# Layer 0 up to three blocks ahead of layer 1, handed out step by step, in half-block streams

## The chip, the cores and the metric

One core of one Trainium2 chip runs the whole program in one launch. The metric is the device time of that launch in microseconds (us), as the median of several runs. PE is the matmul engine, ACT the scalar engine (exponentials, copies with a scale), DVE the vector engine (reductions, elementwise), POOL the GpSimd engine, SP the queue that issues DMAs. SBUF is the on-chip memory that all engines read; PSUM holds eight banks of 128 x 512 fp32 into which PE alone writes its results.

## The reference

The input is x of shape (4, 2048, 256): four sequences ("batches") of 2048 tokens, 256 channels, fp32. Two layers follow each other, each with attention and a feed-forward part, each part added to x:

```python
x = x + attn0(layernorm(x))     # one head, key and value dim 64, biases, causal softmax
x = x + ffn0(layernorm(x))      # clip and round to fp8 (e4m3), to fp16, times W^T, + bias
x = x + attn1(layernorm(x))     # 16 heads of 16, rotary embedding of q and k, causal softmax
x = x + ffn1(layernorm(x))      # xr, xk = mixes of x and x one token earlier
                                # sigmoid(xr Wr^T) * (relu(xk Wk^T)^2 Wv^T)
```

Everything is per token except the two attentions, which look at all earlier tokens of the same sequence, and the last part, which looks one token back. Most of the work is the scores of layer 1: 16 heads, each 2048 x 2048, half of it cut off by the causal mask.

## The kernel before, in words

**Tiling.** A block is 512 tokens (`BLK`). Each of the 4 batches has blocks qb = 0 to 3, so there are 16 blocks in `order`, numbered i. Layer 1's attention goes block by block. The 16 heads form 4 groups g of 4 heads; the four heads of a group sit on the four 32-row strips of PE and run side by side. For one block and group the keys are walked in steps kt of 128 keys: 4, 8, 12 or 16 steps for qb = 0, 1, 2, 3. In all there are 4 x 4 x (4+8+12+16) = 640 such steps, and they are the main loop of the program.

**A step.** `scores` issues twelve matmuls into four PSUM banks (high half of q, low half of q, and the shift by the row maximum, for four heads; on the diagonal also mask matmuls). `exponentials` turns the four banks into probabilities on ACT, two heads at a time. `weighted` multiplies the probabilities of the step before with the values into the bank `av`. `maxima` issues eight matmuls into four more banks for a later group, and four DVE reductions (`reduce_max`, line 612) take their row maxima; a group's maxima must all be done before its scores start, because the softmax shift is a row of the score matmul (`shift_of`). Seven banks of PSUM rotate among scores, maxima and everything else; the eighth is `av`.

**Work beside the steps.** Everything else is written as Python generators that yield after each chunk an estimate of its PE time: `layer0` (layer norm, projections, maxima, scores and values of layer 0 for one block), `layer0_rest` (output projection, fp8 feed-forward, second layer norm and transposes, one generator for each half of the block), `project1` (q, k, v of layer 1, rotary embedding on POOL, split of q and k in high and low parts, transposes) and `layer1_end` (output projection, layer norm, token mix, feed-forward, output DMA). The first three form the list `first` for the next block, i+1, made by `first_part` when block i begins; `layer1_end` of block i-1 goes into the list `end` at the third step of block i. `beside` pulls from `first` while there is any, then from `end`.

**Order.** Python issues all instructions in one sequence, and at the end of `seq_kernel` each engine's instructions are tied to that order, so every engine works through its queue exactly as issued: an instruction that waits holds up all behind it on its engine. Within a step the chunks may come at up to three places, by the rate that is due: after the first two exponentials, after the last two, and behind the maxima. The rate spreads what is left over the remaining steps of the same block:

```python
rate = max(left, 0.0) / max((NG - g) * n - kt - 1, 1)
if first:
    rate = max(rate, early)
credit = min(credit + rate, rate + 2.0)
slots = 3 if rate > 3 else 2 if rate > 1.8 else 1
```

`run_maxima` issues a group's maxima during the group before, two steps ahead; before the first maxima of a new block it pulls what is left of `first` in one go, because those maxima need that block's q and k.

**Buffers.** SBUF tiles named `w2` (128 x 512 fp32, 10 of them) and `w4` (128 x 1024 fp32, 4) serve the chunks, `pT` (4 of 128 x 2 x 512) the probabilities, `x` (3 of 128 x 4 x 256) the activations of a block.

Of the kernel before, what the change touches and what calls it, by code (L numbers as in the profile page):

```python
# [22 lines left out]
P = 128  # L23
# [7 lines left out]
HG = 4  # L31
# [6 lines left out]
W2, W4, PT = 10, 4, 4  # L38


def turns(*gens):

    live = list(gens)
    while live:
        for g in list(live):
            try:
                yield next(g)
            except StopIteration:
                live.remove(g)
# [3 lines left out]
def seq_kernel(  # L53
# [63 lines left out]
    def load_x(b, qb):  # L117
        t = work.tile([P, TT, C], F32, tag="x", name=f"x_{b}_{qb}", bufs=3)
        nc.sync.dma_start(
            t, x_in[b, qb * BLK : (qb + 1) * BLK, :].rearrange("(t p) c -> p t c", p=P)  # L120
        )
        return t
# [82 lines left out]

    def bank(name, dtype=F32):
        cols = BLK * (2 if dtype == F16 else 1)
        return ps.tile([P, cols], dtype, tag="sc", name=name)
# [4 lines left out]
    def w2(name, dtype=F32):  # L213
        return work.tile([P, BLK], dtype, tag="w2", name=name, bufs=W2)
# [4 lines left out]
    def w4(name, more=0):  # L219
        return work.tile([P, CK * (BLK + more)], F32, tag="w4", name=name, bufs=W4)  # L220

    def w4n(name):
        return w4(name).rearrange("p (t c) -> p t c", t=TT)

    def w4t(name):
        return w4(name).rearrange("p (k n) -> p k n", k=CK)
# [3 lines left out]
    def stats(x, hf, tag):  # L230

        mv = small.tile([P, 2, 2], F32, tag="mv", name=f"mv_{tag}_{hf}")
# [6 lines left out]
        y = small.tile([P, 2], F32, tag="y", name=f"y_{tag}_{hf}")  # L239
# [29 lines left out]
    def normal_T(x, dst, hf, tag, copy):  # L269

        my = stats(x, hf, tag)
        yield 0.0
        xn = w2n(f"xn_{tag}_{hf}")
        normalize(x, hf, my, xn)
        yield 0.0
        transpose(xn, dst[:, :, hf * HALF : (hf + 1) * HALF], f"{tag}_{hf}", copy)
        yield 0.6
# [6 lines left out]
    def shift_rows(pad, name):  # L284
# [8 lines left out]
        sh = work.tile([P, BLK], F32R, tag="sh", name=name, bufs=3)  # L293
        nc.scalar.copy(sh, pt)  # L294
        return sh


    kT0, v0 = {}, {}

    def layer0(b, qb, x):  # L300
        tag = f"a0_{b}_{qb}"
        xT = w4t(f"xT_{tag}")
        yield from turns(
            normal_T(x, xT, 0, tag, nc.scalar.copy),
            normal_T(x, xT, 1, tag, nc.vector.tensor_copy),
        )
        kT = kv.tile([P, BLK], F32R, tag="kT0", name=f"kT_{tag}", bufs=NB)
        qh = w2(f"qh_{tag}", F32R)
        ql = w2(f"ql_{tag}", F32R)
        for i in range(2):  # L310
            pq = bank(f"pq_{tag}_{i}")
            for k in range(CK):
                nc.tensor.matmul(  # L313
                    pq, wqk0[:, k, i * P : (i + 1) * P], xT[:, k, :],
                    start=(k == 0), stop=(k == CK - 1),
                )
            hi = (qh, kT)[i]
            lo, r = ((ql, slice(0, P)), (kT, slice(D0, P)))[i]
            nc.scalar.activation(hi, pq, AF.Identity, bias=bqk[:, i : i + 1])
            nc.vector.scalar_tensor_tensor(  # L320
                lo[r, :], pq[r, :], bqk[r, i : i + 1], hi[r, :].bitcast(F32),
                ALU.add, ALU.subtract,
            )
            yield 1.8
        pv = bank(f"pv_{tag}")
        for t in range(TT):
            token_mm(pv[:, t * D0 : (t + 1) * D0], xT, wv0, t)
        va = kv.tile([P, TT, D0 + 1], F32, tag="v0", name=f"v_{tag}", bufs=NB)
        nc.vector.tensor_tensor(
            va[:, :, :D0],  # L330
            pv[:, : TT * D0].rearrange("p (t d) -> p t d", t=TT),
            bv_bc[:, None, :].to_broadcast([P, TT, D0]),
            ALU.add,
        )
        nc.gpsimd.memset(va[:, :, D0 : D0 + 1], 1.0)
        kT0[qb], v0[qb] = kT, va
        yield 1.8


        mx = small.tile([P, TT, NB], F32, tag="mx0", name=f"mx_{tag}")  # L340
        for t in range(TT):
            for kb in range(qb + 1):
# [10 lines left out]
                if kb % 2 or kb == qb:  # L353
                    yield 0.6 * (1 + kb % 2)
# [4 lines left out]
        sh = shift_rows(pads[2], f"sh_{tag}")  # L359
# [5 lines left out]
        for kt in range(nkt + 1):  # L365
            now = None
            if kt < nkt:
                sc = bank(f"s_{tag}_{kt}")
# [13 lines left out]
            if last is not None:  # L382
# [4 lines left out]
                )  # L387
            last = now
            yield 1.6
        cx = w2(f"cx_{tag}")[: D0 + 1, :]  # L390
        nc.scalar.copy(cx, av[: D0 + 1, :])
        ctx0[b, qb] = cx, work.tile(
            [P, CK, BLK], F16, tag="w2", name=f"qhT_{tag}", bufs=W2
        )
        yield 0.0

    ctx0, xT1, ready1 = {}, {}, set()

    def layer0_rest(b, qb, x, hf):

        tag = f"a0_{b}_{qb}"
        while (b, qb) not in ctx0 or (hf == 1 and (b, qb, 0) not in ready1):
            yield None
        cx, qhT = ctx0[b, qb]
        t2 = slice(2 * hf, 2 * hf + 2)
        if hf == 0:
            xT1[b, qb] = w4t(f"xT1_{tag}")
        for t in range(2 * hf, 2 * hf + 2):
# [8 lines left out]
            )  # L417
        my = stats(x, hf, f"f{tag}")
        yield 1.0
        ready1.add((b, qb, hf))  # L420
# [10 lines left out]
        for k in range(CK):  # L431
# [5 lines left out]
        nc.vector.tensor_copy(  # L437
            qhT[:, :, hf * HALF : (hf + 1) * HALF],
            pt[:, :BLK].rearrange("p (k n) -> p k n", k=CK),
        )  # L440
        yield 0.5
        po = bank(f"pof_{tag}_{hf}")
        for j in range(2):
            token_mm(po[:, j * C : (j + 1) * C], qhT, wf16, 2 * hf + j)
# [6 lines left out]
        yield from normal_T(  # L451
            x, xT1[b, qb], hf, f"a1_{b}_{qb}", (nc.scalar.copy, nc.vector.tensor_copy)[hf]
        )
        ready1.add((b, qb, hf, "T"))

    kT1, v1, q1 = {}, {}, {}
    VW = NH * (DK + 1) + SLOT - DK - 1

    def project1(b, qb, x):

        tag = f"a1_{b}_{qb}"
        while (b, qb, 0, "T") not in ready1:
            yield None
        xT = xT1[b, qb]

        va = kv.tile([P, TT, VW], F32, tag="v1", name=f"v_{tag}")
        nc.gpsimd.memset(va, 1.0)
        v1[b, qb] = va  # L470
        H2 = DK // 2
        roped = {}

        def project(t):
            it = qb * TT + t
            pq = bank(f"pq_{tag}_{t}")
            token_mm(pq, xT, wqkv1[:, :, : 2 * C], t)
# [3 lines left out]
            rb = w2(f"rb_{tag}_{t}")  # L481
            rb2 = rb.rearrange("p (h z d) -> p h z d", z=2, d=H2)
            for z, s in ((0, nsin_sb), (1, sin_sb)):
# [8 lines left out]
            nc.gpsimd.tensor_tensor(qk[:, C:], qk[:, C:], rb[:, C:], ALU.add)  # L492
            qd = w2(f"qd_{tag}_{t}")
            nc.gpsimd.tensor_tensor(
                qd.rearrange("p (h z d) -> p h z d", z=2, d=DK),
                *(
                    r[:, :C].rearrange("p (h d) -> p h d", d=DK)[:, :, None, :]
                    .to_broadcast([P, NH, 2, DK])
                    for r in (qk, rb)
                ),  # L500
                ALU.add,
            )
            roped[t] = qk, qd

        def values(t):
            pv = bank(f"pv_{tag}_{t}")
            token_mm(pv[:, :C], xT, wqkv1[:, :, 2 * C :], t)
# [3 lines left out]
            )  # L511

        def halves(t):
            qk, qd = roped[t]
            kn = w2(f"kn_{tag}_{t}", F32R)
# [6 lines left out]
            roped[t] = kn, qd  # L522

        def slots(t):
            kn, qd = roped.pop(t)
            cols = slice(t * P, (t + 1) * P)
            if t == 0:
                kT1[b, qb] = kv.tile([P, NG, BLK], F32R, tag="kT1", name=f"kT_{tag}")
                q1[b, qb] = [
                    [  # L530
# [451 lines left out]
```

## Time and profile before

| | |
|---|---|
| runs | 3714.28, 3714.72, 3714.59 us; median 3714.59 |
| profiled execution | 3709.86 us; span 3707.0 us, mean granted PE clock 0.893 |
| PE busy | 3272.5 us (88%) |
| DVE, ACT, POOL busy | 2068.7 (56%), 1671.8 (45%), 618.0 us (17%) |
| layer 1 score steps | 640; the first starts at 100.7 us |
| line 612, DVE, maxima | 2560 reductions, 1377.5 us |
| line 646, ACT, exponentials | 2560, 1167.1 us |
| line 624, PE, score matmuls | 7680, 1301.8 us in the three groups |
| line 653, PE, probabilities x values | 5120, 663.5 us |

An engine's busy time is the union of its instructions' times. Matmuls overlap in the pipeline, so a group's sum can exceed what it adds to the span. The granted clock is the share of full speed that PE's clock was let run at; in this trace it is at any moment 1.0 or 0.5, so 0.893 means that PE ran at half speed for 21% of the span. A stretch of the span can be asked for its busy times and its clock; the prediction does that block by block.

### The profile page before, as it was taken

What the parts mean: (1) busy time and instruction counts of PE and PEld (TensorE: products, weight loads), DVE (VectorE), ACT (ScalarE), POOL (GpSimd) and SP (SyncE); (2) the same over time, 40 slices, a digit from 0 to 9 for tenths busy, and PEclk for the clock granted to TensorE, in tenths of its full rate; (3) what the DMA queues carried; (4) which work ended last, traced back from release to release, by engine and by line L of the source; (5) the groups of instructions that cost most, each with busy time, mean ns of one, the idle gap of its engine ahead of it and who ended that gap; (6) DMA issues with size and microseconds to landing.
All of it is one profiled execution on the core that took longest, in us unless ns stands there. A gap on an engine that the chain in (4) does not pass through costs nothing.

```text
span 3707.0 us, 73056 instructions
## 1 busy us (share of the span) xinstructions
PE 3272.5 (88%) x31136; PEld 1708.1 (46%) x31136; DVE 2068.7 (56%) x4455; ACT 1671.8 (45%) x3552; POOL 618.0 (17%) x825
## 2 busy tenths in 40 slices
PE   4788898899979899899997979889997888988998
PEld 3454444444445454444454545444444544444444
DVE  3464655667445465656634556456754554646663
ACT  1234444455534444445643434454563434444455
POOL 3212103002030300301203030120211202021001
PEclk8788899799988889989997989998998898999899
DMA  1000000000000000000000000000000000000000
GB/s 52 1 1 1 13 1 1 12 1 2 13 1 12 1 13 1 1 13 2 2 13 1 13 1 13 1 1 13 2 4 10 13 1 4 9 1 7 1 1 12
DMA packets 22903, 24.63 MB, mean 7 GB/s; under 512 B 3953, under 2 KB 22322, under 8 KB 22578
## 3 DMA queue, kind: packets, MB, share of 16 engines
q1 hardware_dynamic: 22578, 19.97, 1.7%
q8 instruction: 244, 4.00, 0.5%
q14 instruction: 81, 0.66, 0.1%
HBM read 11.18 MB, written 8.39 MB: 5 GB/s over the span
## 4 chain that ended last, share of the span: by engine, by line
PE 68%; DVE 24%; ACT 3%; POOL 2%; issue 2%; DMA 0%; POOLq 0%; ACTq 0%; DVEq 0%
DVE mx L612 16%; PE s L624 15%; PE av L653 14%; PE m L599 9%; PE av_a L384 3%; PE pq_a L264 3%; PE pk_f L726 2%; ACT p L646 2%; PE pq_a L313 2%; PE s_a L372 2%; PE pw_f L264 2%; PE pr_f L264 2%; PE s L634 2%; PE pv_a L264 1%; PE m_a L346 1%
## 5 line engine op out<-in xcount | busy, mean ns | idle before, releaser
L612 DVE TENSOR_REDUCE mx<-m 128x1 f32<-128x512 f32 (+3 forms) x2560 | 1377.5, 602 | 932.9 <-PE m L599 594.5
L646 ACT ACTIVATE p<-s 128x512 f32<-128x512 f32 (+3 forms) x2560 | 1167.1, 541 | 1102.4 <-PE s L634 576.6
L624 PE MATMUL s<-qh_a,kT_a 32*128 32x512 f32 (+3 forms) x2560 | 592.0, 482 | 88.3 <-DVE mx L612 70.0
L653 PE MATMUL av<-p,v_a 128*32 128x512 f32 (+3 forms) x5120 | 663.5, 589 | 0.0
L624 PEld LDWEIGHTS s<-qh_a,kT_a 32*128 32x128 f32 x2560 | 267.4, 195 | 426.5 <-DVE mx L612 212.2
L599 PE MATMUL m<-kT_a,qh_a 32*128 32x512 f32 (+3 forms) x2560 | 391.2, 487 | 46.6 <-DVE mx L612 33.3
L599 PEld LDWEIGHTS m<-kT_a,qh_a 32*128 32x128 f32 x2560 | 173.7, 195 | 460.2 <-issue 167.5
L624 PE MATMUL s<-ql_a,kT_a 32*128 32x512 f32 (+3 forms) x2560 | 371.1, 431 | 0.0
L624 PE MATMUL s<-sh,ones 32*128 32x512 f32 (+3 forms) x2560 | 338.7, 395 | 0.0
L599 PE MATMUL m<-kT_a,ql_a 32*128 32x512 f32 (+3 forms) x2560 | 290.7, 394 | 0.0
L238 POOL TENSOR_SCALAR v_fa<-mv_fa 128x2 f32<-128x2 f32 x32 | 7.0, 219 | 1251.2 <-DVE mv_fa L236 1251.2
L624 PEld LDWEIGHTS s<-sh,ones 32*128 32x128 f32 x2560 | 204.4, 205 | 22.7 <-ACT sh L294 5.4
L653 PEld LDWEIGHTS av<-p,v_a 128*32 128x32 f32 x5120 | 108.6, 113 | 181.3 <-issue 161.5
L624 PEld LDWEIGHTS s<-ql_a,kT_a 32*128 32x128 f32 x2560 | 176.0, 203 | 0.0
L599 PEld LDWEIGHTS m<-kT_a,ql_a 32*128 32x128 f32 x2560 | 153.3, 201 | 0.0
L264 PE MATMUL pq_a<-wqkv,xT_a 128*128 128x512 f32 x256 | 140.6, 676 | 4.9 <-ACT xT_a L259 4.9
L384 PE MATMUL av_a<-p_a,v_a 128*65 128x512 f32 (+3 forms) x320 | 144.3, 533 | 0.2
L380 ACT ACTIVATE p_a<-s_a 128x512 f32<-128x512 f32 (+3 forms) x160 | 86.8, 542 | 97.0 <-PE s_a L375 57.5
L258 PE MATMUL pt_a<-ident,xn_a 128*128 128x128 f32 x256 | 55.8, 359 | 73.0 <-DVE xn_a L247 73.0
L634 PE MATMUL s<-maskT_p,ident_p 32*128 32x128 bf16 (+3 forms) x4096 | 119.5, 208 | 0.0
L352 DVE TENSOR_REDUCE mx_a<-m_a 128x1 f32<-128x512 f32 (+3 forms) x160 | 90.6, 604 | 47.2 <-PE m_a L346 41.3
L550 DVE TENSOR_TENSOR ql_a<-pt_a,qh_a 128x256 fp32r<-128x256 f32 x128 | 54.1, 423 | 105.6 <-ACT qh_a L549 105.6
(157 smaller groups left out, 3859.4 us busy)
## 6 DMA issues: line engine op xcount, KB each, us to landing
x<-in_x SPq DMA_DIRECT2D x16, 512.0 KB, 3.9
out_y<-x SPq DMA_DIRECT2D x32, 256.0 KB, 2.1
wqkv<-in_wqkv1T SPq DMA_DIRECT2D x1, 768.0 KB, 8.4
wqk<-in_wqk0T SPq DMA_DIRECT2D x1, 256.0 KB, 4.3
wo<-in_wo1T SPq DMA_DIRECT2D x1, 256.0 KB, 8.6
wr<-in_wrT SPq DMA_DIRECT2D x1, 256.0 KB, 8.8
wk<-in_wkT SPq DMA_DIRECT2D x1, 256.0 KB, 7.4
wv<-in_wvT SPq DMA_DIRECT2D x1, 256.0 KB, 6.0
```

The costliest lines, as they stand in the source:

```text
L264: nc.tensor.matmul(dst, lhsT[:, k, t * P : (t + 1) * P], w[:, k, :], start=(k == 0), stop=(k == CK - 1),)
L313: nc.tensor.matmul(pq, wqk0[:, k, i * P : (i + 1) * P], xT[:, k, :], start=(k == 0), stop=(k == CK - 1),)
L352: nc.vector.reduce_max(mx[:, t, kb : kb + 1], sc[:, :w], axis=AX.X)
L372: nc.tensor.matmul(sc[:, c0:], keys, qh[:, c0:], start=True, stop=False)
L380: nc.scalar.activation(pT[:, c0:], sc[:, c0:], AF.Exp, scale=D0**-0.5)
L384: nc.tensor.matmul(av[: D0 + 1, c:], v0[k // TT][:, k % TT, :], p[:, c:], start=(k == 0), stop=(k == nkt - 1),)
L599: nc.tensor.matmul(scs[h][:, :w], q[r, cols], kT1[b, kb][r, g, :w], start=(q is qh), stop=(kb < qb and q is ql),)
L612: nc.vector.reduce_max(mx[:, t, h, kb : kb + 1], scs[h][:, :w], axis=AX.X)
L624: nc.tensor.matmul(scs[h][:, c0:], ones[r, :] if i == 2 else kT1[b, kt // TT][r, g, kcols], sh[r, c0:] if i == 2 else (qh, ql)[i][r, c0:], ...
L634: nc.tensor.matmul(scs[h][:, c0 : c0 + (v + 1) * SLOT], ident_p[r, v, :], maskT_p[r, v, : (v + 1) * SLOT], start=False, stop=(v == HG - 1),)
L646: nc.scalar.activation(pTs[h // 2][:, h % 2, c0:], scs[h][:, c0:], AF.Exp, scale=DK**-0.5)
L653: nc.tensor.matmul(av[h * SLOT : (h + 1) * SLOT, c0:], v1[b, kt // TT][:, kt % TT, at : at + SLOT], pTs[h // 2][:, h % 2, c0:], start=(kt ...
```

## The change

- **Layer 0 runs ahead.** It is no longer tied to the next block. `a_of` makes its five generators for a block (two halves of `a_in`, `a_mid`, two halves of `a_out`), and `refill` starts the next block whenever the list `A` is empty, up to two blocks beyond the running one, or three once the end of the previous block is through. Before the first step, layer 0 of block 0 is done and that of block 1 partly. There are four `x` buffers.
- **Metering.** A step's credit grows by at least `BASE` = 1.75, more where the deadlines of `rate_of` ask for it. A generator whose chunk yields zero or more is pulled at most once in a step; a negative yield lets it go on in the same step.
- **Place.** All chunks stand behind the step's maxima, none between the exponentials.
- **Half-block streams.** `layer1_end` becomes `end_half`, once for each half; `project1` is split into `b_in`, `b_project`, `b_keys` and `b_queries`. q of layer 1 is kept in one tile `qr` and doubled on POOL (two copies) only when its pair of groups is due.
- **Maxima of a block's first group** are all issued during the last group of the block before, from its first step on; `force(Bq)` completes what they need in that step.
- **Buffers.** 13 `w2` and no `w4`; `pT` is 6 tiles for one head each; copies of transposed tiles are all on ACT.

The diff, cut to its core:

```diff
-W2, W4, PT = 10, 4, 4
+W2, PT = 13, 6
...
-        t = work.tile([P, TT, C], F32, tag="x", name=f"x_{b}_{qb}", bufs=3)
+        t = work.tile([P, TT, C], F32, tag="x", name=f"x_{b}_{qb}", bufs=4)
...
-        transpose(xn, dst[:, :, hf * HALF : (hf + 1) * HALF], f"{tag}_{hf}", copy)
+        if not out_to:
+            out_to.append(w2t(f"xT_{tag}_{hf}"))
+        transpose(xn, out_to[0], f"{tag}_{hf}", nc.scalar.copy)
+        done(1)
         yield 0.6
...
-            yield 1.6
+            yield -1.7
...
-            qd = w2(f"qd_{tag}_{t}")
-            nc.gpsimd.tensor_tensor(
-                qd.rearrange("p (h z d) -> p h z d", z=2, d=DK),
...
+            nc.gpsimd.tensor_tensor(qr1[b, qb][:, t, :], qk[:, :C], rbf[:, :C], ALU.add)
+            roped[b, qb, t] = count[0], qk, rb
+            yield -1.8
...
+    def b_keys(b, qb):
+        for t in range(TT):
+            while (b, qb, t) not in roped or count[0] < roped[b, qb, t][0] + 2:
+                yield None
...
+    def b_queries(b, qb, pair, hf):
...
+        qd = w2(f"qd_{tag}_{hf}")
+        for j in range(2):
+            nc.gpsimd.tensor_copy(
...
-    def layer1_end(b, qb, x, cn):
+    def end_half(b, qb, x, cn, hf):
...
-        for hf in range(2):
-            nc.scalar.activation(sg[:, hf * BLK : (hf + 1) * BLK], prs[hf], AF.Sigmoid)
+        sg = w2(f"sg_{tag}")
+        nc.scalar.activation(sg, pr, AF.Sigmoid)
         yield 1.8
...
-                yield G - 1 + (s + 1) / n - 2 / lead, i
+                yield G - 1 + (s * (lead - 1) // n / lead if g == 0 else (s + 1) / n - 2 / lead), i
...
+    def pull(lists, floor, once=True):
...
+                    if once and used.get(id(gen)) == count[0]:
+                        continue
...
+                    if c >= 0:
+                        used[id(gen)] = count[0]
+                    credit -= abs(c)
...
+    def refill(i):
+        if not A and a_next < min(i + (4 if not E and at[1] > 0 else 3), N):
+            a_load[0] = 0.0
+            A.extend(a_of(a_next))
+            a_next += 1
...
+    def rate_of(i, g, kt, n):
+        to = lambda where: max(where * n - (g * n + kt), 1)
+        rate = BASE
+        first = a_load[0] if a_next == i + 2 else 0.0
+        if first > 0 or Bq:
+            rate = max(rate, first / to(1.5), (first + b_load[0] + e_load[0] / 2) / to(3))
+        return max(rate, (q_load[0] + e_load[0]) / to(4))
...
+    while Bq or Q:
+        credit = 1.0
+        pull([Bq, Q, A], -1e9)
+        pull([A2], -4.0 if A else -6.0)
+        count[0] += 1
...
-            if need >= done_first:
-                pull(first)
+            if need > b_done:
+                force(Bq)
+                b_done = need
...
-            slots = 3 if rate > 3 else 2 if rate > 1.8 else 1
+            refill(i)
+            rate = rate_of(i, g, kt, n)
+            credit = min(credit + rate, rate + 1.5)
             scs, pTs, c0 = scores(b, qb, g, kt, shifts[G])
             exponentials((0, 1), scs, pTs, c0)
-            if slots > 2:
-                beside(credit - rate / 3)
...
             exponentials((2, 3), scs, pTs, c0)
-            if slots > 1:
-                beside(credit - rate / slots)
...
             run_maxima(G + kt / n)
-            beside(0.0, slots)
+            first = A if a_next == i + 2 else None
+            pull([first, E, Bq, Q] if first else [E, Bq, Q, A], 0.0)
         if g == NG - 1:
-            pull(end)
+            force(E)
+            force(Q)
```

## The prediction, made before the changed kernel was run

> **What bounds the kernel now.** I read the page's first two parts, then stretches of the span block by block, then the matmul queue's idle times.
>
> ```profile
> PE 3272.5 (88%) x31136; PEld 1708.1 (46%) x31136; DVE 2068.7 (56%) x4455; ACT 1671.8 (45%) x3552; POOL 618.0 (17%) x825
> ...
> PE   4788898899979899899997979889997888988998
> PEclk8788899799988889989997989998998898999899
> ```
>
> PE is busy 88% and the others about half: PE's queue sets the end. Busy time at half clock counts double, so I take busy time x granted clock as PE's work at full speed, W, and span - W as loss, which is idle time and half clock together. For the span W = 3272.5 x 0.893 = 2922 us and the loss is 785. The next view gives us, busy time of PE, PEld, DVE, ACT and POOL, PE clock, DMA share and GB/s for stretches; first blocks 0 to 3 of batch 2, then the eight groups of blocks 2 and 3 of batch 1.
>
> ```profile
> 1893.00:2051.00 158.00, 125.57 (x1274) 75.93 (x1276) 77.33 (x187) 54.26 (x125) 37.95 (x49) 0.81 0.02 6
> 2051.00:2265.00 214.00, 186.45 (x1772) 99.84 (x1776) 120.71 (x268) 90.01 (x193) 38.50 (x52) 0.87 0.03 8
> 2265.00:2544.00 279.00, 251.66 (x2248) 126.92 (x2248) 160.32 (x328) 123.67 (x261) 38.21 (x49) 0.91 0.02 5
> 2544.00:2798.00 254.00, 246.42 (x2508) 119.21 (x2512) 157.36 (x332) 150.05 (x313) 39.05 (x52) 0.97 0.02 6
> ```
>
> ```profile
> 1360.00:1426.00 66.00, 63.89 (x572) 33.19 (x575) 41.91 (x84) 29.04 (x60) 1.99 (x5) 0.93 0.00 1
> 1426.00:1500.00 74.00, 63.46 (x564) 29.80 (x557) 37.51 (x83) 30.04 (x64) 7.26 (x11) 0.95 0.00 1
> 1500.00:1564.00 64.00, 57.74 (x574) 30.31 (x572) 37.20 (x79) 34.23 (x77) 22.84 (x28) 0.98 0.01 2
> 1564.00:1639.00 75.00, 66.62 (x544) 33.77 (x542) 43.67 (x83) 30.67 (x60) 6.45 (x8) 0.80 0.05 15
> 1639.00:1708.00 69.00, 66.31 (x645) 32.09 (x643) 46.63 (x95) 34.70 (x71) 1.92 (x5) 0.92 0.01 1
> 1708.00:1775.00 67.00, 65.21 (x650) 30.45 (x649) 48.15 (x105) 36.37 (x76) 15.31 (x20) 0.98 0.01 1
> 1775.00:1840.00 65.00, 63.94 (x657) 31.82 (x660) 44.04 (x84) 40.25 (x89) 14.29 (x16) 1.00 0.01 2
> 1840.00:1893.00 53.00, 50.75 (x560) 24.65 (x552) 18.03 (x50) 38.56 (x77) 6.99 (x11) 0.99 0.07 21
> ```
>
> Block 0: W = 125.57 x 0.81 = 102, loss 56 (16 steps, 3.5 us each). Block 1: 162 and 52 (32 steps, 1.6). Block 2: 229 and 50 (48 steps, 1.0). Block 3: 239 and 15 (64 steps, 0.2). So 732 us of work and 173 us of loss; the same sum over the other batches' stretches gives 169, 172 and 182. Loss sits where much chunk work meets few steps. By group, block 2 loses 6.6, 13.7, 7.4 and 21.7 us, block 3 8.0, 3.1, 1.1 and 2.8. The same stretches of batch 2 give block 0 11.3, 20.9, 11.7, 12.0 and block 1 7.4, 15.6, 12.2, 15.3. What happens in a bad one, on PE (start, duration, line, idle before and its releaser in brackets):
>
> ```profile
> 1487.61 0.40 PE L434 MATMUL ptf_a<-ident_h,q_a 128*128 128x128 f16 x4 [1.94 <-POOL q_a L425]
> ...
> 1489.77 1.07 PE L624 MATMUL s<-qh_a,kT_a 32*128 32x128 f32 x2 [1.27 <-DVE mx L612]
> ...
> 1499.58 1.04 PE L264 MATMUL pof_a<-wf,qhT_a 128*128 128x256 f16 x4 [3.10 <-DVE qhT_a L437]
> ```
>
> Links of one layer 0 chain are issued so close that PE waits for POOL and DVE between them; half clock follows (1489 to 1496).
>
> **The change, part by part.**
>
> *Layer 0 ahead, metered, once per step.* PE's work stays; it moves and its chain links come a step (4 to 6 us) apart. In the order in which the changed program issues its matmuls, each taken at its spacing in full-clock parts of the trace (0.47 us for 512 columns of an fp32 record, 0.24 for 256, 0.14 for a transpose), blocks 0 and 1 lose 20 us of chunk work each in batches 1 and 2, block 3 gains 40: W = 82, 142, 229, 279. The longest waits above (3.1, 1.9 us) are shorter than a step, so they end in cover. What is left is the plain step's loss, for which the nearest rows are evenly loaded groups: 0.9 us a step (7.4/8, block 1 g 0), 0.55 and 0.6 (block 2 g 0 and 2), 0.5, 0.2, 0.07 (block 3). I take 0.6 for groups 0 to 2 of blocks 1 and 2 (24 + 36 steps: 14.4 + 21.6), 0.3 for those of block 3 (48: 14.4), and 0.9 for two groups of block 0 (8: 7.2). Group 2 of block 0 still has to catch up (4.9 us of chunks a step in the order of issue): 1.7 x 4 = 6.8. Ends: 0.07 for all 120 steps (8 us) and 1.14 (137 us, the group of 1426).
>
> *Group 3.* Before, it loses 12.0, 15.3 and 21.7 us in blocks 0 to 2. After, all maxima of the next block's first group fall into it (in block 0 three, three, two and none a step; twelve reductions at 602 ns are 7.2 us of DVE), and the leftovers of `b_keys` and `b_queries`, two to four rounds in the order of issue, stand in one piece ahead of the first: PE waits through ACT, DVE and POOL links, and behind it the first maxima and the next scores. Against that, the big chunks leave. I keep 49 us a batch; ends 25 (half) and 64 (5 us more for each of three forced chains). Block 3's own group 3 keeps 2.8.
>
> A batch then loses 14.0 + 14.4 + 21.6 + 14.4 + 49 + 2.8 = 116 instead of 171 (the sum of the groups' figures): -55, over four batches -218. In batch 3 nothing is left to run ahead: groups 1 and 2 of its block 3 stay bare, at 9.0/16 = 0.56 a step as in 3573 to 3637 before, instead of 0.3: +8.
>
> *Start.* The first step came at 100.7 us with W = 42 and 59 of loss, in a chain with waits up to 3.9 us. 27 us of block 1's layer 0 join. I take 50 of loss, the extra work filling some waits: first step at 42 + 27 + 50 = 119 us; -9 of loss. Ends: 101 (all of it in the waits) and 139.
>
> *Sigmoid halves.* ACT loads a table before the sigmoids and before the next exponentials. Before, both sigmoids share a pair of loads:
>
> ```profile
> 1586.91 2.06 ACT L646 ACTIVATE p<-s 128x512 f32<-128x512 f32 x4 [0.29 <-PE s L624]
> 1588.99 1.28 ACT L742 ACT_TABLE_LOAD   x1
> 1590.29 0.60 ACT L742 ACTIVATE sg_f<-pr_f 128x512 f32<-128x512 f32 x1
> ...
> 1593.05 1.28 ACT L646 ACT_TABLE_LOAD   x1
> 1594.34 2.06 ACT L646 ACTIVATE p<-s 128x512 f32<-128x512 f32 x4
> ```
>
> In the changed program they come one at a time: 30 loads more, 38.5 us of ACT. A step's ACT work is about 3 us of 4.6; the load ahead of the exponentials delays the banks that the next maxima need by up to 1.28 us. I take +10 of the ends 0 and 38.5.
> [...]
>
> *What moves between engines, at nothing.* 64 copies go from DVE (683 to 688 ns) to ACT (592): -44 and +38; halved layer 0 and mix operations add about 10 to ACT and 15 to DVE. ACT's cover is its idle 55%, spread over all steps; on the path it would cost 48, DVE's relief could give 29. POOL: qd (64 x 1300) becomes 64 adds at 744 and 128 copies of 256 columns, no row, between 0.3 (a quarter of the 1300 row) and 0.74 (the 256 column add): +3 to +59 us on an engine 17% busy, whose results are used two steps later; uncovered, up to 59. PE: 64 layer 0 projections and 64 of `wk` become pairs of half width; by busy time 506 and 660 ns against 2 x 248 (pw row), -22; by mean durations (631 and 812 against 780), +19; 0 taken. `pT`: exponentials 3 and 4 now wait for two of the eight `av` matmuls (1.07 us together), issued while exponentials 1 and 2 run (1.03 us): 0, up to 0.1 x 640 = 64 if `av` came late. SP: each x load stands behind two more output DMAs (2.1 us) and takes 3.9 us; its first reader is issued five steps or more later; uncovered 6 us a block, 72.
>
> Sum: 3707 - 218 + 8 - 9 + 10 = 3498 us of span; execution +2.9 (3709.86 against 3707.0); the median of the runs stands 4.7 above that execution: **3506 us**, -5.6%.
>
> **The rivals.**
>
> *Bank waits take over: slower.* With all chunks behind the maxima, the next scores take the banks that four reductions free (2.48 us in the trace), against 1.8 us of chunks. For it: idle PE before score matmuls, released by line 612, recurs in plain steps (0.55, 0.67, 1.27 us). Against: groups with as much behind the maxima lose 0.55 to 0.6. If all 120 steps of a batch lose 1.14: 137 + 49 + 3 = 189, +18 a batch; 3707 + 72 + 8 - 9 + 10 + 7.6 = 3796. It decides from 1.0 us a step ((171 - 52)/120).
>
> *Group 3 and the catch-up get worse.* For it: forced chains at the start of every group 3 of blocks 0 to 2, tripled maxima on DVE. Against: the same work waited there before. 80 instead of 49 a batch, and 3 instead of 1.7 in block 0's group 2: +36 a batch, 3650.
>
> *All stalls were chains.* 0.3 us in every step, group 3 at 30: 36 + 30 + 3 = 69 a batch, -408: 3316. For it: block 3's 0.07 to 0.2. Against: those steps carry one chunk, not two.
>
> *The waits only move:* within 0.2% of 3714.59 (7 us, about what a measurement tells from no change), if the half-width streams meet the same links in one step.
>
> **How the numbers follow.** Forecast 0.52 (its own range 3420 to 3590), group 3 worse 0.2, all chains 0.12, no change 0.03, bank waits 0.13. Faster 0.84, same 0.03, slower 0.13. From 3310, below the best case, to 3700 the range leaves out 0.16 and takes in the start (-18 to +20), the tables (-10 to +28) and group 3's ends (-96 to +60).
>
> **What would show it.** Batches 1 and 2, blocks 0 to 3, near 108, 172, 272 and 296 us (158, 214, 279, 254 before); the clock at or above 0.93 outside group 3; waits for `q_a`, `qhT_a` and `xn_a` before PE below a third; the first step near 119 us; ACT table loads near 61. Wrong if blocks 0 and 1 keep their spans, if idle PE before line 622's scores grows past 1 us a step, or if the new block 3 loses more than the others gain.

## The result, and the profile after

The changed kernel takes 3469.51 us (median of four runs, 3466.47 to 3472.42); the kernel before takes 3714.65 us beside it. The ratio is 0.934 (95% interval 0.9324 to 0.9356): 6.6% faster, where 5.6% was forecast (3506 us, range 3310 to 3700). The profiled execution took 3472.42 us; its span is 3470.6.

The page of the changed kernel, busy time by engine and the tenths in 40 slices:

```profile
PE 3179.8 (92%) x31392; PEld 1736.6 (50%) x31392; DVE 2045.0 (59%) x4439; ACT 1801.8 (52%) x3678; POOL 634.7 (18%) x985
...
PE   3799999999998999999999899899999899989998
...
PEclk9899899989997999989999799998999899998899
```

TensorE is now busy 92% of the span at a clock of 0.928 (88% at 0.893 before). In the prediction's terms, with the clock before rounding, W is 2950 us and the loss 521; before they were 2923 and 784 (2922 and 785 in the prediction). So the whole gain is lost time; the work did not shrink. The first slice has a 3 where there was a 4: that is the start.

Stretches, columns as in the prediction: blocks 0 to 3 of batch 2, each from its first score matmul to that of the next block.

```profile
1831.00:1948.30 117.30, 101.72 (x1195) 67.05 (x1194) 66.23 (x162) 52.98 (x118) 37.24 (x55) 0.85 0.03 10
1948.30:2114.20 165.90, 155.80 (x1705) 88.20 (x1704) 114.44 (x245) 88.42 (x185) 31.19 (x50) 0.97 0.03 8
2114.20:2380.00 265.80, 245.35 (x2282) 127.69 (x2280) 158.71 (x340) 136.96 (x275) 44.04 (x68) 0.93 0.02 5
2380.00:2670.70 290.70, 281.52 (x2683) 143.20 (x2682) 170.79 (x361) 172.44 (x343) 44.76 (x68) 0.96 0.02 5
```

117, 166, 266 and 291 us, against 158, 214, 279 and 254 before: blocks 0 and 1 gave up 89 us, block 2 13, and block 3 took 37.

What TensorE waited for (in total, times, longest):

```profile
PE pt_a L252 <- DVE xn_a L241: 57.8, 5, 50.8
PE pt_a L575 <- POOL qd_a L558: 34.6, 5, 9.9
PE s L622 <- DVE mx L610: 30.2, 71, 1.9
...
PE pk_a L537 <- DVE rb_a L528: 17.0, 10, 3.5
...
PE ptf_a L445 <- POOL q_a L436: 13.2, 13, 3.0
```

The longest in the kernel before:

```profile
PE pt_a L258 <- DVE xn_a L247: 73.0, 23, 22.0
PE s L624 <- DVE mx L612: 70.0, 177, 1.4
PE pk_a L538 <- DVE kn_a L519: 63.4, 40, 3.7
PE ptf_a L434 <- POOL q_a L425: 40.9, 26, 3.7
PE pof_a L264 <- DVE qhT_a L437: 34.9, 12, 4.6
PE m L599 <- DVE mx L612: 33.3, 43, 2.3
```

Of the 57.8 us for `xn_a`, 54.0 fall in the start, 50.8 of them in one wait; behind the first step 3.8 are left of 44.7. The links that the prediction blamed are small: `q_a` 13.2 us (40.9 before), and `qhT_a` is no longer listed (34.9 before). `rb_a` is the tile that was `kn_a`: 17.0 us of 63.4. These signs came as the prediction said, if the start is left out of `xn_a`; so did the 62 table loads (61 forecast, 32 before). The clock is 0.97, 0.93 and 0.96 in blocks 1 to 3, but in batch 2 three groups ahead of group 3 are clearly below the 0.93 that the prediction named: 0.90, 0.89 and 0.88 in group 2 of block 0, group 0 of block 1 and group 1 of block 2.

### The profile page after: what moved, and what is told of

It is laid out like the page before. It is cut to its first block, busy times and chain, and to the rows that moved or that the text cites. A ratio compares the mean times of both kernels' runs of the same rounds, so it can differ in the third digit from the quotient of the medians.

```text
span 3470.6 us, 75157 instructions
## 1 busy us (share of the span) xinstructions
PE 3179.8 (92%) x31392; PEld 1736.6 (50%) x31392; DVE 2045.0 (59%) x4439; ACT 1801.8 (52%) x3678; POOL 634.7 (18%) x985
## 4 chain that ended last, share of the span: by engine, by line
PE 71%; DVE 17%; ACT 5%; POOL 3%; issue 3%; SPq 1%; DMA 0%; POOLq 0%; ACTq 0%; DVEq 0%
PE s L622 16%; PE av L651 15%; PE m L597 11%; DVE mx L610 11%; PE av_a L398 3%; PE pq_a L258 3%; ACT p L644 2%; PE pv_a L258 2%; PE pk_f L721 2%; PE po_f L258 2%; PE s_a L386 1%; PE pw_f L258 1%; PE s L632 1%; PE pq_a L318 1%; PE pt_c L662 1%
## 5 line engine op out<-in xcount | busy, mean ns | idle before, releaser
L644 ACT ACTIVATE p<-s 128x512 f32<-128x512 f32 (+3 forms) x2560 | 1206.2, 533 | 1009.2 <-PE s L622 517.0
L622 PE MATMUL s<-qh_a,kT_a 32*128 32x512 f32 (+3 forms) x2560 | 539.2, 475 | 60.8 <-DVE mx L610 30.2
L597 PE MATMUL m<-kT_a,qh_a 32*128 32x512 f32 (+3 forms) x2560 | 465.4, 488 | 60.2 <-ACT p L644 28.2
L597 PEld LDWEIGHTS m<-kT_a,qh_a 32*128 32x128 f32 x2560 | 207.8, 194 | 573.6 <-issue 154.0
L622 PEld LDWEIGHTS s<-qh_a,kT_a 32*128 32x128 f32 x2560 | 244.3, 189 | 412.7 <-DVE mx L610 120.4
L622 PE MATMUL s<-ql_a,kT_a 32*128 32x512 f32 (+3 forms) x2560 | 338.0, 407 | 0.0
L597 PE MATMUL m<-kT_a,ql_a 32*128 32x512 f32 (+3 forms) x2560 | 328.8, 410 | 0.0
L622 PE MATMUL s<-sh,ones 32*128 32x512 f32 (+3 forms) x2560 | 310.5, 378 | 0.0
L605 PE MATMUL m<-mask_p,ident_p 32*128 32x128 bf16 (+3 forms) x4096 | 107.3, 205 | 0.0
L632 PE MATMUL s<-maskT_p,ident_p 32*128 32x96 bf16 (+3 forms) x4096 | 105.9, 199 | 0.0
```

The source lines that it names most:

```text
L597: nc.tensor.matmul(scs[h][:, :w], q[r, cols], kT1[b, kb][r, g, :w], start=(q is qh), stop=(kb < qb and q is ql),)
L605: nc.tensor.matmul(scs[h][:, w - P + v * SLOT : w], ident_p[r, v, :], mask_p[r, v, v * SLOT :], start=False, stop=(v == HG - 1),)
L622: nc.tensor.matmul(scs[h][:, c0:], ones[r, :] if i == 2 else kT1[b, kt // TT][r, g, kcols], sh[r, c0:] if i == 2 else (qh, ql)[i][r, c0:], ...
L632: nc.tensor.matmul(scs[h][:, c0 : c0 + (v + 1) * SLOT], ident_p[r, v, :], maskT_p[r, v, : (v + 1) * SLOT], start=False, stop=(v == HG - 1),)
L644: nc.scalar.activation(pTs[h][:, c0:], scs[h][:, c0:], AF.Exp, scale=DK**-0.5)
```

## Where the prediction stood, term by term

Loss in us, by the same groups of steps; "after" is the mean of batches 1 and 2 (103.6 and 101.3).

| | before | forecast | after |
|---|---|---|---|
| block 0, groups 0 and 1 | 31.9 | 7.2 | 1.3 |
| block 0, group 2 | 10.9 | 6.8 | 6.8 |
| block 1, groups 0 to 2 | 36.8 | 14.4 | 11.6 |
| block 2, groups 0 to 2 | 28.1 | 21.6 | 22.1 |
| block 3, groups 0 to 2 | 12.1 | 14.4 | 15.1 |
| group 3 of blocks 0 to 2 | 48.9 | 49 | 40.8 |
| group 3 of block 3 | 2.9 | 2.8 | 4.8 |
| a batch | 171.4 | 116 | 102.5 |
| start, to the first step | 59.0 | 50 | 85.6 |
| first step at | 100.7 | 119 | 153.8 |

All batches together lose 406 us against 483 in the forecast, the start 36 more than forecast, and W is 28 higher. The start is the term that failed, outside its own ends (101 and 139). The experiments take it first, then the reason given for the even steps, then running ahead, then the terms that were taken near zero.

## The experiments

All are made from the changed kernel, except the one marked. The last column is (ratio - 0.934) x 3714.65 us; each ratio is known to about 0.0015, or 6 us, so differences under some 8 us say nothing.

| what | median, us | ratio to before (95%) | against the changed kernel |
|---|---|---|---|
| x of block 1 loaded early | 3442.8 | 0.9277 (0.9262 to 0.9292) | -23 |
| chunks of one stream may follow in a step | 3743.9 | 1.009 (1.0069 to 1.011) | +279 |
| half of each step's credit ahead of the maxima | 3761.3 | 1.0136 (1.0116 to 1.0157) | +296 |
| the kernel before, chunks behind the maxima only | 3712.3 | 1.0013 (1.0003 to 1.0022) | |
| layer 0 one block ahead | 3603.5 | 0.9714 (0.9695 to 0.9732) | +139 |
| layer 0 two blocks ahead | 3447.3 | 0.9297 (0.9282 to 0.9313) | -16 |
| no sigmoid, no table loads | 3436.5 | 0.925 (0.9234 to 0.9266) | -33 |
| doubling copies on VectorE | 3450.2 | 0.9291 (0.9276 to 0.9307) | -18 |
| edge copies on ScalarE | 3475.4 | 0.9353 (0.9339 to 0.9367) | +5 |
| early x and doubling copies | 3427.3 | 0.9242 (0.9228 to 0.9255) | -36 |
| early x, doubling and edge copies | 3410.5 | 0.918 (0.9166 to 0.9194) | -59 |
| these three, projections due earlier | 3405.0 | 0.9187 (0.9172 to 0.9202) | -57 |

### The start: x of block 1 loaded early

VectorE and TensorE at the start of the changed kernel (start, duration, engine, line, idle before and its releaser):

```profile
49.29 0.43 DVE L229 BATCH_NORM_STATS2 st_a<-x 128x6 f32<-128x256 f32 x1 [28.45 <-DMA x<-in_x]
...
50.82 2.56 PE L252 MATMUL pt_a<-ident,xn_a 128*128 128x128 f32 x8 [50.82 <-DVE xn_a L241]
```

The statistics of block 1 are issued straight after those of block 0. They wait 28.45 us for a load that stands on SP behind all weight and mask loads, and block 0's own normalization is queued behind them, so TensorE's first matmul comes at 50.82 us.

```diff
-    xs = {order[0]: load_x(*order[0])}
+    xs = {o: load_x(*o) for o in order[:2]}
...
-        if i > 0:
+        if i > 1:
             xs[b, qb] = load_x(b, qb)
```

> The load of block 1's x is issued directly behind that of block 0, ahead of the weights; nothing else is changed. Theory: the start grew because VectorE's first statistics of block 1 stand right behind those of block 0 and wait 28.45 us for a load that is queued on SP behind every weight and mask load; then that wait falls below 3 us, the first step comes at about 125 us instead of 153.8, and the time falls by 25 to 30 us, to about 3442. Rival: the start is long because block 1's layer 0 adds its own work to the chain; then the wait goes, but other waits take its place, the first step stays above 145 us, and the time falls by less than 9 us.

TensorE's first matmul, and the start as a stretch, with the load early:

```profile
23.15 2.24 PE L252 MATMUL pt_a<-ident,xn_a 128*128 128x128 f32 x8 [23.15 <-DVE xn_a L241]
```

```profile
0.00:125.60 125.60, 77.33 (x432) 53.75 (x432) 53.87 (x148) 28.70 (x55) 47.14 (x88) 0.86 0.14 43
```

The wait is gone, the first step comes at 125.6 us, and the time falls by 23 us. The start loses 59.1 us, as much as before the change (59.0). Block 1's work that the start took over is in W (67 us instead of 42), where the forecast had it. So the whole excess over the kernel before was this one load. Of the 36 us over the forecast it explains 27; the other 9 are waits that the extra work was to fill, and did not.

### The even steps: spacing and place

```diff
-            pull([first, E, Bq, Q] if first else [E, Bq, Q, A], 0.0)
+            pull([first, E, Bq, Q] if first else [E, Bq, Q, A], 0.0, once=False)
```

> Undoes the spacing alone: chunks of one stream may follow one another within a step again, as far as the step's credit goes. Theory: a chunk whose predecessor ran in an earlier step finds its input ready, and this spacing is what took away the waits of TensorE for layer 0's q_a and qhT_a; without it these waits come back to some 20 to 40 us and the time rises by 30 to 80 us. Rival: the credit per step (1.75 to 3 units, one or two chunks) spaces the streams by itself; then the time stays within 10 us.

TensorE's waits in this kernel:

```profile
PE pt_a L252 <- DVE xn_a L241: 178.4, 41, 51.1
PE ptf_a L445 <- POOL q_a L436: 51.9, 23, 4.0
PE pk_f L721 <- DVE mix_f L711: 41.5, 12, 7.5
PE pk_a L537 <- DVE rb_a L528: 31.5, 13, 3.5
```

All gain is lost and more: the time is 0.9% above the kernel before. Waits inside chains that were 7 us (`xn_a` without its one wait of 51 us), 13 (`q_a`), 2 (`mix_f`) and 17 (`rb_a`) are 127, 52, 42 and 32. That is the mechanism by which the prediction let the long waits end. The size was three and a half times the upper end of what I expected: the rate alone does not space the links, since by the code one generator may take the whole credit of a step, and a chunk that yields zero takes none of it.

```diff
             exponentials((2, 3), scs, pTs, c0)
             last = now
+            first = A if a_next == i + 2 else None
+            pull([first, E, Bq, Q] if first else [E, Bq, Q, A], credit - rate / 2)
```

> Half of each step's credit is pulled behind the exponentials and ahead of the maxima, the rest behind the maxima as now. Theory: work put ahead of the maxima delays the reductions on VectorE and the banks that they give back, so that steps lose 0.1 to 0.3 us each (640 steps) and the time rises by 60 to 190 us. Rival: the place inside a step is worth nothing because the queues even it out; then the time stays within 10 us.

Groups and waits; a group's tail is busy time and mean of one, then the idle time ahead. The changed kernel, then this one:

```profile
L622 PE MATMUL s<-qh_a,kT_a 32*128 32x512 f32 (+3 forms) x2560 | 539.2, 475 | 60.8 <-DVE mx L610 30.2
```

```profile
L622 PE MATMUL s<-qh_a,kT_a 32*128 32x512 f32 (+3 forms) x2560 | 731.6, 471 | 207.5 <-DVE mx L610 167.4 <-DVE ql_a L582 5.8 <-DVE kT_a L325 3.7
```

```profile
PE s L622 <- DVE mx L610: 167.4, 288, 5.4
```

Scores wait 167 us for the maxima's reductions instead of 30, in 288 places instead of 71. The busy time of these matmuls rises too, from 539.2 to 731.6 us at the same mean of one (475 and 471 ns): they overlap less, as they would when the four heads' banks come free one after another; that reason is argued, not shown. So the chunks behind the maxima are what TensorE does while VectorE reduces. In the prediction this place was the ground of a rival, "bank waits take over". The sign was wrong: idle time ahead of the scores, released by the maxima, fell from 70 us to 30, which is 0.05 us a step, far from the 1.0 at which that rival decides.

Is the place worth as much by itself? In the kernel before, with the same edit alone:

```diff
-            if slots > 2:
-                beside(credit - rate / 3)
...
-            if slots > 1:
-                beside(credit - rate / slots)
```

> The kernel before, with one part of the change alone: the chunks that it pulls between the exponentials and ahead of the maxima in steps of a high rate are left out there, so that all chunks stand behind the step's maxima, as many rounds of them as before. Theory: the place is worth much by itself; TensorE's waits for the maxima (70 us ahead of the scores, 33 ahead of the next maxima) fall below 60 us together and the time falls by 30 to 120 us. Rival: the place pays only together with spaced half-block streams; here two or three chunks of one stream now follow one another, the waits inside the chains (xn, kn, q and qhT, 212 us together) grow to 250 us or more, and the time is the same or up to 100 us longer.

TensorE's waits in this kernel (those of the kernel before stand above; `xn_f` was 14.6):

```profile
PE pt_a L258 <- DVE xn_a L247: 102.9, 27, 22.7
PE pk_a L538 <- DVE kn_a L519: 75.5, 40, 3.7
...
PE pt_f L258 <- DVE xn_f L247: 28.8, 8, 4.3
PE s L624 <- DVE mx L612: 27.4, 92, 0.6
...
PE m L599 <- DVE mx L612: 20.3, 39, 1.6
```

The maxima's waits fall by 56 us as the theory said, but the time does not fall (+0.1%): chains wait more. The rival is right on the time, though the waits that it counted sum to 228 us and not to 250. So, as far as these runs go, the place pays only with spaced streams, and the spaced streams only with the place. Their prices, 279 and 296 us, are each larger than the whole gain of 245, so neither can be read as a share of it.

### Running ahead

```diff
-        if not A and a_next < min(i + (4 if not E and at[1] > 0 else 3), N):
+        if not A and a_next < min(i + 2, N):
...
         if g == 0 and i + 1 < N:
+            refill(i)
             b_of(i + 1)
```

> Undoes the running ahead alone: inside the loop layer 0 is created for one block ahead at most, where the changed kernel goes up to three. Half-block streams, metering and places stay. Theory: running ahead lets the long blocks carry layer 0 of the short ones, so without it blocks 0 and 1 have to take 2 to 4 units more per step and their lost time comes back: the loss of a batch goes from about 101 us to 115 to 135 us, most of it in blocks 0 and 1, and the time rises by 50 to 130 us. Rival: the half-block streams and their spacing are the whole cause, and running ahead is worth under 15 us.

Blocks 0 to 3 of batch 2 with one block ahead:

```profile
1840.80:1991.70 150.90, 125.00 (x1286) 82.18 (x1285) 76.70 (x191) 61.26 (x134) 39.22 (x60) 0.85 0.03 8
1991.70:2196.50 204.80, 190.37 (x1785) 109.59 (x1784) 118.06 (x264) 97.55 (x200) 39.52 (x60) 0.88 0.02 6
2196.50:2456.70 260.20, 246.62 (x2261) 129.87 (x2260) 158.16 (x331) 133.54 (x268) 39.51 (x60) 0.92 0.02 5
2456.70:2721.50 264.80, 254.40 (x2521) 126.42 (x2520) 152.34 (x323) 159.89 (x320) 39.48 (x60) 0.93 0.02 5
```

Blocks 0 and 1 take 73 us more than in the changed kernel, block 3 gives back 26. The loss of this batch goes from 101 to 141 us. The theory holds in size, at a little more than the upper end of its price, but not in place: of the 36 us that blocks 0 and 1 lose more, 30 stand in their group 3 (35.5 and 19.0 us instead of 21.2 and 3.7), where what is left is forced, and only 6 in the steps ahead of it, which take more work. Without running ahead 106 us of the gain remain. Beside the spacing and the place these hold parts of the change that no run undoes by themselves: the half-block streams, the buffers, the copies of transposed tiles on ScalarE and the early maxima of a block's first group.

```diff
-        if not A and a_next < min(i + (4 if not E and at[1] > 0 else 3), N):
+        if not A and a_next < min(i + 3, N):
```

> The changed kernel with layer 0 at most two blocks ahead instead of three (one block ahead cost 134 us). Theory: the third block is needed, since block 3, with 64 steps, would otherwise run out of layer 0 (it can hold that of blocks 0 and 1, but not that of block 2) and blocks 0 and 1 would have to make up for it; then the time is 30 to 80 us longer, with the loss in the even steps of blocks 0 and 1. Rival: two blocks ahead already let the short blocks go without layer 0 work of their own; then the time is within 15 us of the changed kernel.

Blocks 0 to 3 of batch 2 with two blocks ahead:

```profile
1797.70:1912.30 114.60, 103.17 (x1211) 69.29 (x1210) 69.26 (x163) 54.58 (x122) 31.83 (x50) 0.90 0.03 11
1912.30:2110.30 198.00, 185.88 (x1803) 106.61 (x1802) 124.96 (x274) 96.92 (x200) 39.35 (x60) 0.92 0.02 7
2110.30:2354.90 244.60, 237.66 (x2275) 122.90 (x2273) 156.33 (x336) 135.07 (x274) 39.96 (x62) 0.96 0.02 6
2354.90:2630.50 275.60, 263.12 (x2566) 132.38 (x2567) 161.75 (x338) 162.75 (x326) 47.25 (x69) 0.93 0.02 5
```

The theory missed: two blocks ahead are 16 us faster than three. The rival's 15 us are met within the noise, on the faster side. Block 1 is 32 us longer, but blocks 2 and 3 are 21 and 15 shorter. Span less loss gives the work: the third block ahead moves 20 us of it from block 1 (171 to 151) to block 3 (246 to 271), and block 2 has 227 or 228 in both. But block 2 loses 38 us with three and 17 with two, 16.7 against 1.3 in its group 1, where layer 0 and the block end meet on POOL (below). That is more than block 1's loss fell by, 26 to 15. Block 0 loses 7 us more with three, and block 3 10 less.

### The terms taken near zero

Table loads of ScalarE in the changed kernel:

```profile
L736 ACT ACT_TABLE_LOAD x31 | 39.8, 1283 | 2.3 <-PE pr_f L258 1.7
...
L644 ACT ACT_TABLE_LOAD x29 | 37.2, 1283 | 6.6 <-PE s L622 3.3 <-PE s L632 3.1
```

```diff
-        nc.scalar.activation(sg, pr, AF.Sigmoid)
+        nc.scalar.activation(sg, pr, AF.Relu)
```

> The sigmoid of the block ends is replaced by a Relu, which leaves the sigmoid out of the computation and with it all 60 table loads of ScalarE (77 us of its time); everything else stays. Theory: the trace shows the loads beside TensorE's work, so most of them cost nothing; by the share taken in the forecast (10 of 38.5 us for the 30 loads that the change added) all 60 cost about 20 us, and the time falls by 5 to 35 us. [...]

33 us for 60 loads of 1283 ns is 0.56 us each, so the 30 that the change added cost, at that mean, about 17 us of their 38.5; I had taken 10. The trace of the changed kernel has 77 us of loads with 9 us of idle time ahead of them.

Group 3 of block 0 was the group that got worse, 21.2 us instead of 11.8 in batch 2. The group as a stretch, and its first wait in the changed kernel:

```profile
1906.80:1948.30 41.50, 30.23 (x325) 19.92 (x324) 22.31 (x46) 11.80 (x28) 12.78 (x19) 0.67 0.06 20
```

```profile
1915.80 1.24 PE L575 MATMUL pt_a<-ident,qd_a 128*128 128x128 f32 x4 [7.48 <-POOL qd_a L558]
```

In those 7.48 us POOL does the rotary products of the same step's projection, two doubling copies, then layer 0's casts and bias additions, and only then the doubling copies for which TensorE waits. I had covered POOL by "17% busy, whose results are used two steps later"; a forced stream has no two steps.

```diff
-            nc.gpsimd.tensor_copy(
+            nc.vector.tensor_copy(
                 qd[:, j * 2 * P : (j + 1) * 2 * P].rearrange("p (h z d) -> p h z d", z=2, d=DK),
```

> The doubling copies of the queries (128 of 407 ns) move from POOL to VectorE. Theory: in group 3 of block 0 the forced queries wait 7.5 us for POOL, which has rotary work queued ahead, and the start waits 9.9 us for it as well; on VectorE both waits fall below 3 us, TensorE's waits for these copies (38 us in 15 waits) fall under 15 us, and the time falls by 15 to 35 us. Rival: VectorE's queue is as long there, and its 0.4 us per copy stands ahead of the maxima in 128 places; then the waits only change their name and the time changes by less than 6 us, or rises.

TensorE's waits for these copies:

```profile
PE pt_a L575 <- DVE qd_a L558: 6.6, 12, 1.0
```

34.6 us become 6.6, the group loses 14.4 us in batch 2 instead of 21.2, and the time falls by 18 us: the theory holds. One row that I had only bounded, 0.3 to 0.74 us for a copy on POOL, is 407 ns.

The next largest loss was group 1 of block 2, 16.7 us, where ScalarE's mixing waits 7.2 us for a copy of one column on POOL. The group as a stretch, and that wait:

```profile
2174.80:2248.10 73.30, 64.08 (x575) 34.22 (x574) 42.22 (x99) 35.48 (x71) 12.64 (x20) 0.88 0.02 5
```

```profile
2219.02 1.71 ACT L708 ACTIVATE mix_f<-xs_f,omu_sb 128x256 f32<-128x256 f32 x4 [7.17 <-POOL xs_f L699]
```

Layer 0's casts and additions are ahead of that copy too, and not the rotary products that I named.

```diff
-            nc.gpsimd.tensor_copy(xs_[:, :, 0:1], edges.pop((b, qb - (1 - hf), 1 - hf)))
+            nc.scalar.copy(xs_[:, :, 0:1], edges.pop((b, qb - (1 - hf), 1 - hf)))
...
-        nc.gpsimd.tensor_copy(edges[b, qb, hf], xs_[:, :, HALF : HALF + 1])
+        nc.scalar.copy(edges[b, qb, hf], xs_[:, :, HALF : HALF + 1])
```

> The two copies of the edge column in a block end move from POOL to ScalarE. Theory: in group 1 of block 2 the step stands because ScalarE's mixing waits up to 7.2 us for POOL, whose queue has the rotary products ahead of the copy; without that the group's lost time falls from 16.7 to under 10 us and the time by 10 to 30 us. Rival: that wait only becomes a wait for the chunks' own work on ScalarE and VectorE; then the group stays within 3 us and the time within 6 us.

The group falls to 7.8 us as forecast, and the time does not fall. It is given back mainly in group 3 of block 1, 3.7 to 10.9 us. That group, here and in the changed kernel:

```profile
2067.20:2118.90 51.70, 48.13 (x437) 26.12 (x436) 37.77 (x75) 16.10 (x35) 0.00 (x0) 0.85 0.01 1
```

```profile
2067.50:2114.20 46.70, 42.96 (x433) 23.16 (x432) 37.60 (x75) 15.83 (x35) 0.00 (x0) 1.00 0.01 1
```

Idle time is the same, 3.6 and 3.7 us. The clock is 0.85 instead of 1.00, and that is the difference.

The combinations:

> The early load of block 1's x and the doubling copies on VectorE, without the move of the edge copies. Theory: the move of the edge copies changed nothing by itself (+6 us), so the three together got their gain from these two: about 3412 us, within 6 of the three together. Rival: the edge copies on ScalarE pay once the other two waits are gone: 3423 us, the sum of the two single gains (27 and 19), or more.

> The early load of block 1's x, the edge copies on ScalarE and the doubling copies on VectorE together. Theory: the three remove waits in different places (start; group 1 of block 2; group 3 of block 0), so their gains add: 27 us of the early load (measured) plus those of the other two, 3380 to 3420 us in all. Rival: they share one cause, the credit that is pulled in those groups, and removing one wait uncovers the next; then the sum of the three is missed by over 15 us.

Early load and doubling copies together give 36 us, about the sum of the two (41). The edge copies, worth nothing alone, then give 23 more, so of the pair's expectations the rival holds. The three reach the 3380 to 3420 us of their theory, but not by its reason: the single gains sum to 37 us, and they gave 59. Group 1 of block 2 falls here as it did alone (to 8.0 us in batch 2), and group 3 of block 1, which gave that back, loses 6.7, where the pair loses 8.5. Why the clock holds there in this order and not in the other stays open.

```diff
-            rate = max(rate, first / to(1.5), (first + b_load[0] + e_load[0] / 2) / to(3))
+            rate = max(rate, first / to(1.5), (first + b_load[0] + e_load[0] / 2) / to(2.25))
```

> The three edits together as before, and in addition the projections of the next block are due after 2.25 groups instead of 3. Theory: what is left of group 3's loss (14 us per batch in block 0, 15.9 in block 2, 6.7 in block 1) comes from projections that are still open when group 3 starts (four streams in blocks 0 and 2) and are then pulled through without spacing; with an earlier due time nothing is left there, the loss of group 3 in blocks 0 and 2 falls by 6 to 10 us each, and the time falls by 25 to 60 us against the three edits. Rival: the same work then crowds groups 0 to 2, whose steps take two chunks instead of one; their loss rises by as much and the time stays within 12 us.

Group 3 of block 0 falls only from 14.0 to 11.4 us in batch 2; batch 2 loses 6 us less and batch 0 14 more; the ratio is the same. In batch 2 groups 0 to 2 lose 6 us more and group 3 of block 2 only 4.5 less, so the rival holds on the time. The three edits alone are as good: 3410.5 us, 8.2% below the kernel before.

## Why the prediction was right, and where not

- **Even steps, 0.6 us (0.3 in block 3): right in sum, wrong in kind.** Blocks 1 to 3 came within 3 us of their terms. But there is no such plain step. Of the 108 steps of these groups in batch 2, 76 lose under 0.2 us and the median step nothing; 13 steps lose over 1 us each and hold 37 of the 47 us (before, 21 held 61 of 73). What the change left is fewer stalls, and that they come to 0.6 a step is luck. That chains which step apart took the others away is shown by the 279 us that they cost without the spacing. It was half of the reason: the place behind the maxima was needed as well, and I had counted it as a risk only.
- **Two groups of block 0 at 0.9:** 0.16 was measured.
- **Group 3 kept at 49:** 40.8 in sum, by cancelling: block 0 +9.2 (the forced chain), block 1 -11.6, block 2 -5.8. The sum is luck.
- **Start, -9:** the step that failed is "each x load ... its first reader is issued five steps or more later". For blocks 2 to 15 no reader waits for its load in the trace. Block 1's first reader is issued in the prologue, right behind block 0's, and waits 28.45 us. +27 us of loss instead of -9; the hope that extra work fills waits of the start failed too.
- **Table loads, +10:** about 17.
- **W unchanged:** +28 against the forecast. The start took over 26 us of W, and the batches did not get lighter by it. The work also moved less far: blocks 0 to 3 of batch 2 have 89, 151, 228 and 271 us, not 82, 142, 229 and 279. The halved matmuls now have rows: 256 of 446 ns for `wk` against 128 of 812, and 256 of 414 for layer 0's projections against 128 of 631, which is +35 us by mean durations and -5 by busy time. (By its own rows the prediction's sum of mean durations is +15, not +19.) Whether these are the 28 us is not shown.
- **The sum** came 36 us lower than forecast: batches -77 and their table loads -10, start +36, W +28, tail and rounding -4, and the median stood 1 below the profiled span instead of 8 above, -9.
- **Rivals:** bank waits fell by more than half; group 3 did not get worse in sum; a batch loses 102 us and not the 69 of "all stalls were chains", which rests on an even loss in every step like the forecast.

## What to carry to other kernels

Metering work between the steps of a main loop pays by two rules together, one link of a chain per step and the filler where another engine's result is awaited; either alone gave nothing or lost the whole gain here. When work is moved into a prologue, follow its first load through the DMA queue: its position among the other loads cost 28.45 us of wait here, and the fix was two lines worth 23 us. Give filler enough room that the largest stage is not its only place, and try less lookahead too: here two blocks beat three. Look at the loss step by step before taking a mean: a few stalls can hold most of it.

## What the runs showed of the hardware

The clock went two ways behind the same idle time. TensorE in group 3 of block 1, with the edge copies on ScalarE:

```profile
2070.35 0.98 PE L597 MATMUL m<-kT_a,qh_a 32*128 32x512 f32 x3 [0.49 <-ACT p L644]
...
2071.18 2.20 PE L622 MATMUL s<-qh_a,kT_a 32*128 32x512 f32 x4
2072.60 1.21 PE L622 MATMUL s<-ql_a,kT_a 32*128 32x512 f32 x4
...
2075.21 1.94 PE L651 MATMUL av<-p,v_a 128*32 128x512 f32 x8
```

and in the changed kernel:

```profile
2070.58 0.98 PE L597 MATMUL m<-kT_a,qh_a 32*128 32x512 f32 x3 [0.48 <-ACT p L644]
...
2071.41 1.90 PE L622 MATMUL s<-qh_a,kT_a 32*128 32x512 f32 x4
2072.82 0.72 PE L622 MATMUL s<-ql_a,kT_a 32*128 32x512 f32 x4
...
2074.28 1.06 PE L651 MATMUL av<-p,v_a 128*32 128x512 f32 x8
```

After idle times of 0.49 and 0.48 us the same matmuls run at half clock in the one (1.94 us for eight `av`) and at full clock in the other (1.06 us). In the trace of the changed kernel half the clock is granted for 502 us of the span (791 before). All but one of its 65 stretches last a multiple of 3.4 us, up to 27.3, and all its changes of clock fall within 1 ns on one grid of 3413.33 ns. In the 3.4 us ahead of a half-clock stretch TensorE was busy for 66% in the median. The busy share alone does not decide the clock: from the first step on, 92 periods of that grid that ran at full clock were busy for less than 90%, one for only 48%, and the full clock stayed behind them. In the pair above the period ahead of the half clock was 83% busy, and the one with the same idle time in the changed kernel 86%. What decides stays open. So a wait of half a microsecond has no fixed price: here the step behind it took 7.7 us or 11.6.
